# Preparation of the next block in thirds, and dequantisation gathered at the end of a layer, in a four-layer hybrid kernel

## The chip, the cores and the metric

The kernel runs on one core of one Trainium2 chip. The metric is the device time of one execution in microseconds (us): the median of the runs shown. A core has TensorE (PE, matrix products; its weight loads are listed apart as PEld), VectorE (DVE), ScalarE (ACT), GpSimd (POOL) and SyncE (SP, which here only issues DMAs). Each engine runs its own instructions in the order in which the program gives them, and they meet through semaphores. PE writes only PSUM; SBUF holds all other tiles.

## What is computed

One sequence of 2048 tokens with 256 channels in float32 goes through four layers, each added to its input after a layer norm: attention a, a gated MLP, attention b, the same MLP again.

```python
x = x + attn_a(layernorm(x))   # 16 heads of 16, 4 key/value heads, rotary angles, biases, causal
x = x + ffn(layernorm(x))      # gate, up: 256 -> 2048, gelu(gate) * up, down: 2048 -> 256
x = x + attn_b(layernorm(x))   # 16 heads of 16, 16 key/value heads, no bias, causal
x = x + ffn(layernorm(x))      # the same weights
```

The MLP's three weight matrices come packed, one 4-bit code pair to an int32 and one scale for each 32 values, and are expanded in the kernel once, for both MLP layers:

```python
low, high = W_packed & 15, W_packed >> 4 & 15
vals = NVFP4_LUT[stack([low, high], -1).reshape(N, -1)]
W = (vals.reshape(N, K // 32, 32) * scales[:, :, None]).reshape(N, K)
```

## The kernel before

**Blocks and units.** The tokens are cut into four blocks of 512 (`NB`), the 16 heads into four groups of four (`NG`). An attention layer is a sequence of 16 units, block by block and in each block the groups 0 to 3; unit (b, g) works out softmax(scores) times values for the queries of block b and the heads of group g (`value_steps`, main steps: one for each key tile of 128 and each pair of heads, so 8, 16, 24 or 32 steps in block 0, 1, 2 or 3). A main step adds the negated row maximum to the scores in PSUM (L853), adds the scores (L858), has ACT take the exponential (L870), and one step later PE multiplies by the values (L838).

**The max pass.** The row maxima must be known before. While unit n runs its main steps, `max_steps` computes the scores of unit n+1 a first time (L758) and DVE reduces them (L770), 9, 17, 25 or 33 steps for a unit of block 0, 1, 2 or 3. So the fourth unit of a block already scores the next block's first group, which needs that block's queries, and in its last steps its keys. The layer's last unit has no unit after it and no max pass.

**Side steps.** `weave` runs main steps and a list of side steps together: after each main step as many side steps as keep the two lists level, with the last three main steps kept free of them. The side list is the max pass blended with `more`, a list that `run` composes for every unit:

- the output projection of the block before (`out_steps`, four steps, in a block's first unit);
- preparation of the next block (`prep_steps(b + 1)`): layer norm (statistics, root on POOL, four normalised tiles `xn`), in the first layer the rotary tables (copied by POOL, L481, turned by PE, L492), the transposes of x (`turn_x`, L466), then projections in column blocks c of 128. In the first layer each rotated block is one product with the weights and one with the swapped weights (L500), each multiplied by its table on DVE (L514), added on POOL (L519), split into a high half (ACT copy, L550) and a low half (DVE, L558), both written to DRAM by SP (L557, L561). Keys come back through eight POOL DMAs (`load_k`, L705), queries through eight SP DMAs for a group (`load_q`, L719). Values go from PSUM to their tile (`keep_value`). This is 31 steps in the first layer and 27 in the second;
- in the first layer dequantisation (`dequant_steps`, handed to `run` as `extra`): 12 tiles of six steps, 72 in all: `load` (codes by SP, L330; scales in eight POOL DMAs, L339), `lowest` (POOL takes the low bytes, L344), two `move`s (DVE bit operations, L355 to L361) and two `scaled` (DVE, L370). Each of their tiles has one buffer, so a load of scales waits for the previous tile's last `scaled`. The first eight tiles fill `wg` and `wu`; the last four are the down projection, which SP writes to DRAM (L399) and the MLP loads again as `wd`;
- in the last unit, `beside`: the 13 steps that prepare block 0 of the MLP (layer norm, then four transposes of `xn`, L1007, copied to `xnT` by ACT, L1008). They come behind everything else in the list.

**Space.** PSUM has three double banks `ps_s` for scores, one bank `ps_av` for the sums of a unit, and one bank `ps_m` that all side products, the transposes and the turned maxima share. Query tiles have three buffers.

**What goes where before the change.** Preparation is cut into 13, 13 and 5 steps (first layer) or 11, 11 and 5 (second) for the units g = 0, 1, 2 of a block. Dequantisation goes in equal shares of six steps, one whole tile, to each of the 12 units of blocks 1 to 3, as a run ahead of the unit's preparation steps. Each unit issues at its start the query load of the unit two ahead.

Of the kernel before, what the change touches and what calls it, by code (L numbers as in the profile page):

```python
# [27 lines left out]
NG = NH // 4  # L28
# [3 lines left out]
NB = S // TB  # L32
# [10 lines left out]
def weave(main, side, rest=0):  # L43


    done = 0
    for n, step in enumerate(main):
        first, *second = step if isinstance(step, tuple) else (step,)
        first()
        want = min(len(side), -(-(n + 1) * len(side) // max(1, len(main) - rest)))  # L50
        while done < want:
            side[done]()
            done += 1
        for f in second:
            f()
    while done < len(side):
        side[done]()
        done += 1


def blend(a, b):

    keyed = [((n + 0.5) / len(a), 0, n, f) for n, f in enumerate(a)]
    keyed += [((n + 0.5) / len(b), 1, n, f) for n, f in enumerate(b)]
    return [f for *_, f in sorted(keyed, key=lambda k: k[:3])]


def cut(steps, n):

    while 0 < n < len(steps) and getattr(steps[n - 1], "open", False):  # L70
        n += 1
    return steps[:n], steps[n:]
# [8 lines left out]
def tile_hybrid_layers(  # L81
# [84 lines left out]
    for src, at in ((bq, 0), (bk, D), (bv, D + 64)):  # L166
        n = src.shape[1]
# [239 lines left out]
    class Attention:  # L407
# [535 lines left out]
        def run(self, extra, beside):  # L943


            units = [(b, g) for b in range(NB) for g in range(NG)]
            per_unit = -(-len(extra) // (len(units) - NG))
            ending, ahead = [], []
            for n, (b, g) in enumerate(units):
                lead, more = [], []  # L950
                if g == 0 and b > 0:
                    more += self.out_steps(b - 1)
                if g == 0 and b + 1 < NB:
                    ahead = self.prep_steps(b + 1)

                    few = -(-(len(ahead) - (6 if self.first else 5)) // 2)
                if n >= NG:
                    more, extra = more + extra[:per_unit], extra[per_unit:]
                if g < 3:
                    part, ahead = cut(ahead, few)  # L960
                    more += part
                if n == 0 and self.after:
                    lead, more = self.after[:2], self.after[2:] + more
                elif n + 2 < len(units):
                    self.load_q(*units[n + 2])
                maxima, turn = [], None
                if n + 1 < len(units):
                    maxima, turn = self.max_steps(*units[n + 1])
                else:
                    more += beside  # L970
                steps, end, divide = self.value_steps(b, g)

                for at, step in zip((0, 2), ending):
                    scored, *summed = steps[at] if isinstance(steps[at], tuple) else (steps[at],)
                    steps[at] = (scored, step, *summed)
                if turn:
                    scored, summed = steps[-1]
                    steps[-1] = (turn, scored, summed)
                first = len(maxima) * 3 // len(steps)
                weave(steps[:3], lead + maxima[:first])  # L980
                weave(steps[3:], blend(maxima[first:], more) if maxima else more, rest=3)
                ending = [end, divide]
            end()
            return [divide] + self.out_steps(NB - 1)
# [197 lines left out]
```

## Time and profile before

| | |
|---|---|
| median of 3 runs | 1878.29 us (1876.99 to 1888.44) |
| the profiled execution, its own time | 1879.59 us |
| its span, first to last instruction | 1877.8 us |
| mean granted PE clock | 0.988 |
| first attention layer, 16 units | 39.7 to 627.8 us |
| second attention layer, 16 units | 986.3 to 1534.7 us |

Times in a view count from the span's first instruction. The granted clock is the share of PE's full speed that the chip's throttle allowed in a stretch; it takes the values 1 and 0.5 here, so a mean of 0.98 over a stretch says that a small part of it ran at half speed. "Busy" of an engine is the time with an instruction of it under way; matmuls overlap, and their ends are modelled.

### The profile page before, as it was taken

How to read it: one execution, taken by the hardware profiler on the slowest of the kernel's cores; microseconds unless marked ns; L12 is line 12 of the kernel's file. 1: busy time of each engine (PE TensorE's matmuls, PEld its weight loads, DVE VectorE, ACT ScalarE, POOL GpSimd, SP SyncE). 2: the span in 40 equal slices, each digit the busy share in tenths (PEclk: the TensorE clock that was granted, in tenths of full speed). 3: DMA queues.
4: the chain of work that ended last, by engine and by line, in shares of the span. 5: the costliest groups of instructions: out<-in, count | busy, mean ns of one | idle time of the engine just before them, and what ended most of it. 6: DMA issues, size and time to landing. Idle time of an engine off the chain costs nothing. (4 is left out here: it accounts for less than half of the span.)

```text
span 1877.8 us, 31994 instructions
## 1 busy us (share of the span) xinstructions
PE 1774.6 (95%) x13534; PEld 928.5 (49%) x13534; DVE 1123.9 (60%) x1679; ACT 806.6 (43%) x1071; POOL 239.1 (13%) x444
## 2 busy tenths in 40 slices
PE   8788988999999999999998898999999999999999
PEld 4343444444444465646464444444444444756656
DVE  4566788688885354353544667766877716353443
ACT  1244445455667422232314355556566663131221
POOL 4211411300001011012101010010000001011110
PEclk9899999999999999999999899999999999999999
DMA  5320410310101100003204132041000010000000
GB/s 136 74 58 24 79 41 23 63 35 24 35 24 36 46 6 1 0 1 72 52 0 91 46 72 54 13 81 41 17 13 2 2 46 1 12 3 9 6 6 12
DMA packets 41887, 63.45 MB, mean 34 GB/s; under 512 B 13712, under 2 KB 20752, under 8 KB 41488
## 3 DMA queue, kind: packets, MB, share of 16 engines
q1 hardware_dynamic: 33104, 45.41, 8.6%
q0 software_dynamic: 7680, 15.48, 5.0%
q8 instruction: 106, 1.74, 0.4%
q10 hardware_dynamic: 960, 0.52, 0.1%
q14 instruction: 37, 0.30, 0.1%
HBM read 43.45 MB, written 17.83 MB: 33 GB/s over the span
## 5 line engine op out<-in xcount | busy, mean ns | idle before, releaser
L770 DVE TENSOR_REDUCE mx<-ps_s 128x2 f32<-128x1024 f32 (+3 forms) x640 | 658.7, 1060 | 220.0 <-PE ps_s L733 112.1
L870 ACT ACTIVATE e<-ps_s 128x1024 f32<-128x1024 f32 (+3 forms) x640 | 571.7, 898 | 423.4 <-PE ps_s L858 242.8
L838 PE MATMUL ps_av<-e,v 128*32 128x256 f32 (+1 forms) x4608 | 363.4, 384 | 0.4 <-ACT e L870 0.4
L858 PE MATMUL ps_s<-qT,kT 64*128 64x512 f32 (+3 forms) x1280 | 338.9, 522 | 0.0
L758 PE MATMUL ps_s<-kT,qT 64*128 64x512 f32 (+3 forms) x1280 | 268.2, 421 | 46.1 <-DVE mx L770 24.2
L853 PE MATMUL ps_s<-mT,sel 64*128 64x512 bf16 (+3 forms) x1280 | 231.0, 355 | 27.5 <-ACT mT L812 11.0
L1031 PE MATMUL ps_s<-xnT,wg 128*128 128x512 f32 x512 | 240.9, 593 | 0.0
L1031 PE MATMUL ps_s<-xnT,wu 128*128 128x512 f32 x512 | 240.6, 592 | 0.0
L758 PEld LDWEIGHTS ps_s<-kT,qT 64*128 64x128 f32 x1280 | 128.6, 187 | 151.9 <-ACT e L870 68.5
L853 PEld LDWEIGHTS <-sel 64*128 64x128 bf16 x1280 | 74.7, 93 | 251.6 <-issue 242.5
L1039 DVE TENSOR_TENSOR t<-ps_s,t 128x512 f32<-128x512 f32 x128 | 88.1, 688 | 158.8 <-POOL t L1038 156.7
L1037 ACT ACTIVATE t<-ps_s 128x512 f32<-128x512 f32 x128 | 76.2, 596 | 244.3 <-PE ps_s L1031 243.9
L1040 ACT ACTIVATE t<-t 128x512 f32<-128x512 f32 x128 | 80.5, 629 | 199.1 <-DVE t L1039 199.1
L1031 PEld LDWEIGHTS ps_s<-xnT,wu 128*128 128x128 f32 x512 | 97.3, 190 | 122.5 <-issue 122.5
L1038 POOL TENSOR_SCALAR t<-t 128x512 f32<-128x512 f32 x128 | 79.1, 618 | 565.4 <-ACT t L1037 564.9
L838 PEld LDWEIGHTS ps_av<-e,v 128*32 128x32 f32 x4608 | 94.6, 108 | 107.2 <-issue 91.7
L1031 PEld LDWEIGHTS ps_s<-xnT,wg 128*128 128x128 f32 x512 | 95.1, 190 | 104.2 <-issue 102.5
L1041 DVE SCALAR_TENSOR_TENSOR t<-t,ps_s 128x512 f32<-128x512 f32 x128 | 88.1, 688 | 88.9 <-ACT t L1040 88.9
L858 PEld LDWEIGHTS ps_s<-qT,kT 64*128 64x128 f32 x1280 | 129.5, 197 | 0.0
L1056 PE MATMUL ps_m<-wd,inter 128*128 128x256 f32 x512 | 114.5, 380 | 0.0
L1056 PE MATMUL ps_av<-wd,inter 128*128 128x256 f32 x512 | 114.5, 380 | 0.0
L1056 PEld LDWEIGHTS ps_av<-wd,inter 128*128 128x128 f32 x512 | 96.7, 190 | 17.1 <-issue 4.5
(145 smaller groups left out, 1201.3 us busy)
## 6 DMA issues: line engine op xcount, KB each, us to landing
qT<-h SPq DMA_DIRECT2D x248, 64.0 KB, 2.2
kT<-h POOLq DMA_DIRECT2D x88, 128.0 KB, 6.0
h<-high SPq DMA_DIRECT2D x24, 256.0 KB, 2.4
h<-low SPq DMA_DIRECT2D x24, 256.0 KB, 3.0
wd<-wd_kept SPq DMA_DIRECT2D x2, 2048.0 KB, 8.4
wd_kept<-dq_d SPq DMA_DIRECT2D x4, 512.0 KB, 3.0
out<-x SPq DMA_DIRECT2D x16, 128.0 KB, 1.7
x<-x SPq DMA_DIRECT2D x3, 512.0 KB, 7.3
```

Of the source, the lines that this page charges most:

```text
L758: nc.tensor.matmul(pt[:, r, :w], lhsT=self.qT[b, g][64 * r : 64 * r + 64, p, i * P : (i + 1) * P], rhs=self.key_rows(c, g, p, r, slice(0, w)),
L770: nc.vector.tensor_reduce(held["mx"][:, i, 2 * p : 2 * p + 2, c], pt[:, :, :w], AX.X, ALU.max)
L838: nc.tensor.matmul(held["av"][32 * j : 32 * j + 32, own], lhsT=self.vv[kt // NT][:, kt % NT, h * VW : h * VW + 32], rhs=es_[j // 2][:, j % ...
L853: nc.tensor.matmul(pt[:, r, q0:], lhsT=sel[64 * r : 64 * r + 64, p, :], rhs=self.mT[b, g][64 * r : 64 * r + 64, q0:], start=True, stop=False,)
L858: nc.tensor.matmul(pt[:, r, q0:], lhsT=self.key_rows(kt // NT, g, p, r, keys), rhs=self.qT[b, g][64 * r : 64 * r + 64, p, q0:], start=Fals ...
L870: nc.scalar.activation(e[:, :, q0:], pt[:, :, q0:], AF.Exp, scale=QK_SCALE)
L1031: nc.tensor.matmul(pt[:, k, :], lhsT=w[:, c, fc * P : (fc + 1) * P], rhs=self.xnT[b][:, c, :], start=(c == 0), stop=(c == 1),)
L1038: nc.gpsimd.tensor_scalar(t, t, GELU_A, 1.0, ALU.mult, ALU.add)
L1039: nc.vector.tensor_tensor(t, gate, t, ALU.mult)
L1040: nc.scalar.activation(t, t, AF.Tanh, scale=GELU_C)
L1041: nc.vector.scalar_tensor_tensor(t, t, 1.0, gate, ALU.add, ALU.mult)
L1056: nc.tensor.matmul(po[:, :D], lhsT=inter[:, fc, i * P : (i + 1) * P], rhs=wd[:, fc, :], start=(fc == 0), stop=(fc == NFC - 1),)
```

## The change

The edit is in `run` of the attention class alone.

- The preparation of the next block is cut into thirds: 8 or 9 steps in unit g = 0 (8 in block 0), 11 in g = 1, the rest, 11 or 12, in g = 2, in the first layer; 7 or 8, 11 or 10, and 9 in the second.
- The query load of unit (b + 1, 0) is no longer issued at the start of unit (b, 2), since the queries are now made in that unit: it stands as a step of its own after the sixth preparation step there.
- Dequantisation is shared by weights: none in block 0, 2 for each unit of blocks 1 to 3, but 0 for the fourth units of blocks 1 and 2, and 9 for the layer's last unit. Worked out, the 12 units of blocks 1 to 3 get 6, 5, 5, 0; 6, 5, 5, 0; 6, 5, 5, 24 steps. A tile's six steps may now lie in two units.
- The unit's share is blended into the list of preparation and output steps instead of standing ahead of it.

```diff
             units = [(b, g) for b in range(NB) for g in range(NG)]
-            per_unit = -(-len(extra) // (len(units) - NG))
-            ending, ahead = [], []
+            room = [0 if n < NG else 9 if n + 1 == len(units) else 2 * (g < 3 or b + 1 == NB)
+                    for n, (b, g) in enumerate(units)]
+            shares = [-(-len(extra) * sum(room[: n + 1]) // sum(room)) for n in range(len(units))]
+            given, ending, ahead = 0, [], []
             for n, (b, g) in enumerate(units):
                 lead, more = [], []
                 if g == 0 and b > 0:
                     more += self.out_steps(b - 1)
                 if g == 0 and b + 1 < NB:
                     ahead = self.prep_steps(b + 1)
-                    few = -(-(len(ahead) - (6 if self.first else 5)) // 2)
-                if n >= NG:
-                    more, extra = more + extra[:per_unit], extra[per_unit:]
-                if g < 3:
-                    part, ahead = cut(ahead, few)
+                    third = len(ahead) / 3
+                    few = [round(third) - (1 if b else 2), round(third) + 1, len(ahead)]
+                if g < 3 and b + 1 < NB:
+                    part, ahead = cut(ahead, few[g])
+                    if g == 2:
+                        part[6:6] = [lambda b=b: self.load_q(b + 1, 0)]
                     more += part
+                if shares[n] > given:
+                    more = blend(more, extra[given : shares[n]])
+                    given = shares[n]
                 if n == 0 and self.after:
                     lead, more = self.after[:2], self.after[2:] + more
-                elif n + 2 < len(units):
+                elif n + 2 < len(units) and g != 2:
                     self.load_q(*units[n + 2])
```

## The prediction

> **What bounds the kernel now.** I write unit (b, g) for the value pass of block b, head group g; a layer has 16, and each starts where ACT copies the previous unit's sums out of PSUM (L885). First the page's busy times and its row of slices:
>
> ```profile
> PE 1774.6 (95%) x13534; PEld 928.5 (49%) x13534; DVE 1123.9 (60%) x1679; ACT 806.6 (43%) x1071; POOL 239.1 (13%) x444
> ...
> PEclk9899999999999999999999899999999999999999
> ```
>
> PE is busy 95% of the span. The change moves work and removes none, so at most it can shift PE's idle time and the half-clock stretches; the question is which units have some. So I cut both attention layers into stretches (view of busy time by window; columns: window, length, then PE, PEld, DVE, ACT, POOL busy, granted clock, DMA share, GB/s). Units (1,0) to (1,2), (2,0) to (2,2) and the last, (3,3), of the first layer:
>
> ```profile
> 132.90:237.10 104.20, 91.08 (x920) 44.82 (x919) 71.89 (x122) 48.60 (x65) 26.24 (x45) 0.98 0.26 54
> ...
> 268.30:403.20 134.90, 124.30 (x1256) 58.06 (x1255) 99.57 (x146) 72.66 (x88) 26.42 (x45) 1.00 0.20 42
> ...
> 590.20:627.80 37.60, 37.12 (x405) 14.87 (x402) 6.65 (x23) 30.69 (x38) 1.04 (x1) 1.00 0.04 15
> ```
>
> The same two stretches of the second layer, whose preparation is lighter and which has no dequantisation:
>
> ```profile
> 1068.40:1159.10 90.70, 85.41 (x906) 43.24 (x903) 59.53 (x89) 48.61 (x66) 9.16 (x17) 1.00 0.32 65
> ...
> 1188.80:1313.20 124.40, 118.54 (x1240) 57.43 (x1239) 87.58 (x113) 73.15 (x90) 9.17 (x17) 1.00 0.22 48
> ```
>
> PE's idle time is length less PE: 13.1 and 10.6 us in the first layer, 5.3 and 5.9 in the second. In (3,3) PE idles 0.5 and DVE 31: there PE sets the pace. The fourth units (1,3) and (2,3), each first in layer 1, then in layer 2:
>
> ```profile
> 237.10:268.30 31.20, 25.78 (x298) 12.69 (x297) 28.38 (x40) 14.77 (x19) 4.42 (x9) 1.00 0.13 35
> 1159.10:1188.80 29.70, 25.21 (x298) 12.61 (x297) 26.04 (x32) 14.76 (x20) 0.00 (x0) 1.00 0.07 17
> 403.20:444.70 41.50, 36.53 (x410) 17.23 (x409) 37.75 (x48) 23.03 (x28) 4.62 (x9) 1.00 0.10 27
> 1313.20:1353.00 39.80, 36.52 (x410) 17.05 (x409) 35.47 (x40) 22.91 (x27) 0.00 (x0) 1.00 0.05 13
> ```
>
> Here DVE is busy nearly throughout (28.38 of 31.20): the next block's longer max pass. Last, what PE waits for in (1,0) to (1,2) (us, times, longest):
>
> ```profile
> PE ps_s L758 <- ACT e L870: 3.1, 5, 1.2
> PE ps_s L758 <- DVE mx L770: 2.4, 3, 1.1
> PE ps_m L500 <- DVE r L514: 1.5, 2, 0.8
> ```
>
> Exponentials behind other ACT work, max reductions behind other DVE work, and the single `ps_m` bank. All three come from side steps set too densely.
>
> **Part A, no dequantisation in (1,3) and (2,3).** After the edit these units hold what their twins of the second layer hold, so they take the twins' length: 31.20 - 29.70 = 1.5 and 41.50 - 39.80 = 1.7. **-3.2**. DVE loses 2.34 and 2.28 busy, so -4.6 is the lower end, 0 the upper. Late next: the max reductions themselves, which stay.
>
> **Part B, thirds, blocks 1 and 2 of the first layer.** Before, unit g=1 held 13 preparation steps, eight using `ps_m`, g=2 five (two). Now it is 9, 11 and 11 steps, and preparation uses `ps_m` seven times in g=1 and five in g=2. Dequantisation, which stood in a lump ahead of them, is mixed in. PE's instructions are the same. At best idle falls to the second layer's level: 23.7 - 11.2 = -12.5. I take a little over half, **-7**, since the heavier preparation (swapped columns, tables) stays. Upper end +3: a load of scales is eight issues on POOL, 3.97 us, and can stand ahead of POOL's add L519, for which ACT's copy L550 waits with the next exponentials behind it. By the lists the copy comes three or more main steps (over 5 us) after each such load, and the eight key loads (0.51 each, 4.1) no longer wait in line for their DRAM write, made a unit earlier; so I keep near the gain. The query load's eight issues leave the head of g=2 for its middle; in SP's queue they now stand behind the halves' writes, with ten or more us to spare in blocks 1 and 2.
>
> **Part C, block 0 of both layers, and the second layer's thirds.** Block 0's units have 8 main steps, and all side work lands in two of them, wherever it is moved; idle there is 15.1 us of 72.2 (first layer) and 8.1 of 60.0. In the second layer two transposes of x leave g=0, one projection leaves g=1; its six other units idle 11.2, of which about 1 each is the fixed wait for mT and o. **-2** for all of it; ends -7, and +10 (second rival). Block 3's units g=0 to 2 go from 18 dequantisation steps to 16, beside DVE's 29 us of idle: 0.
>
> **Part D, the last unit.** By the new shares unit (3,3) gets 24 of the 72 steps, four whole tiles, against one before; ahead of the MLP's own 13 steps, in the same 26 main steps. DVE has 31 us free and four tiles cost it 4 x 2.7. But tiles of a stage have one buffer each, so the four go one after the other. One tile's round, from POOL's and DVE's timelines (start, length):
>
> ```profile
> 582.94 3.97 POOL L339 DMA_DIRECT2D dq_s<-down_s  x8 [41.23 <-DVE dq_d L370]
> 588.19 0.61 POOL L344 COPY dq_b<-dq_q 128x512 uint8<-128x512 uint8 x1 [1.28 <-DMA dq_q<-down_p]
> ```
>
> ```profile
> 581.96 0.68 DVE L370 SCALAR_TENSOR_TENSOR dq_d<-dq_e,dq_s 128x512 f32<-128x512 fp8e4 x1
> ...
> 592.18 0.21 DVE L355 TENSOR_SCALAR dq_t<-dq_b 128x128 uint32<-128x128 uint32 x1
> ...
> 593.56 1.29 DVE L370 SCALAR_TENSOR_TENSOR dq_d<-dq_e,dq_s 128x512 f32<-128x512 fp8e4 x2
> 594.78 0.42 DVE L295 BATCH_NORM_STATS2 stats<-x 128x6 f32<-128x256 f32 x1
> ...
> 598.36 1.38 DVE L310 TENSOR_SCALAR xn<-x,mv,rstd 128x256 f32<-128x256 f32 x4 [1.16 <-POOL rstd L302]
> ```
>
> From the last scaling's start (581.96) to the next tile's unpacked bytes (588.80) it takes 6.84; from there to its own last scaling 2.0 (592.18 to 594.17). Period: 8.8. The first tile is loaded ahead and ends as it does now, last scaling at T+3.97 (T = 590.2); the fourth starts its last at T+30.4; statistics 0.6 later; the first normalised x 4.0 after that: **T+35.0**. PE now reaches the transposes of it (L1007) here:
>
> ```profile
> 616.46 0.50 PE L1007 MATMUL ps_m<-ident,xn 128*128 128x128 f32 x2
> ...
> 620.38 0.34 PE L853 MATMUL ps_s<-mT,sel 64*128 64x384 bf16 x2
> ```
>
> With 37 side steps in place of 19 the first transpose moves from main step 24 to 27, the one that starts at 620.38; less the two transposes that no longer precede it (0.9) and plus its scores (0.45), PE stands there at T+29.75. It waits about **5.0** for DVE, with all later scores and the MLP's first matmuls queued behind. Two transposes now share that step and one bank: +0.9. And the clock: in 176.87 to 180.28 PE was busy 1.82 of 3.41 us, and the next 3.41 ran at 0.50; a stall of 5 us leaves at least one such window emptier than that. Half clock for 3.4 to 6.8 us over a stretch where PE sets the pace costs 1.7 to 3.4: +2.5. **+8.4**; ends 0 and +13 (landings at their longest, 4.6 and 5.0). The write of the last down tile and the 2 MB load of `wd` slip by 27 us, but the first down projection comes some 60 us after the unit.
>
> [...]
>
> **Sum.** -3.2 - 7 - 2 + 8.4 = -3.8 on the profiled execution's 1879.59 (span 1877.8): 1875.8. That execution stands 1.3 above the median of the runs, so **1874.5**.
>
> **Rivals.** *The clock holds through the stall*: D is 5.9, 1872, inside the forecast's own range (0.12 of its chance): for it the window 1542.18 to 1545.59, PE busy 1.99, with the next at 1.00; against it the emptier one above.
> *The last unit hides it all* (chance 0.15): if a round takes 7.06 or less, x is ready at T+29.75 and nothing of D is paid: 1874.5 - 8.4 = 1866. For it: DVE's 31 idle us, and landing rows as short as 1.9. Against: two rounds in the trace are 8.65 and 8.85, mostly fixed issues.
> *Thirds give nothing* (0.18): the idle moves from g=1 to g=2 along with `ps_m`'s users; B and C are 0: 1883.5, slower. For it: the three waits above are local to a step, not to a unit.
> *Block 0's queries come late* (0.10): (0,2) loads what (0,3) scores at once. Modelled on (0,1), where the low half (81.0) was followed by key loads, add and next halves up to the write at 89.5, then 3.0 landing, four issues of 0.46 and 2.2 landing: 15.6 us after it, U+20.5 in a unit of about 22 whose successor reads at U+23. It decides if a landing is over 2.5 us longer than its median; the query rows reach 8.0. Then 3.4 us of stall and 1.7 of half clock, in both layers: +10, 1884.5, slower.
> That the change doesn't do what it says shows only in the word "mostly": a third of the dequantisation goes to the last unit.
>
> **The numbers.** The forecast (1868 to 1881) has 0.50; 0.07 lies outside all of these. The range reaches from the first rival with part of B's best (1862) to D's upper end or the slower rivals with a little more (1888). About 1%, 18.8 us, is what a measurement of this kernel can tell from no change; no case passes it without two bounds at once: faster 0.04, within 0.89, slower 0.07.
>
> **What would show it.** A: (1,3) and (2,3) at 29.7 and 39.8. B: idle of the two first-layer stretches near 16 to 17 in all. D: PE waiting several us for xn at L1007 near the end of the last unit, the clock at 0.5 behind it, POOL's eight issues starting every 8.8 us. C: the first L758 of (0,3) waiting for qT or not. The prediction is wrong if the rounds overlap, if clock windows in block 0 fall differently (each 3.4 us there costs up to 1.7), or if mixing slows the max reductions in the first three units.

## The result

| | before | changed |
|---|---|---|
| median (9 runs each, side by side) | 1882.21 us | 1869.66 us |
| range of the runs | 1876.99 to 1889.71 | 1865.59 to 1874.91 |
| the profiled execution | 1879.59 (granted clock 0.988) | 1874.91 (0.983) |

The ratio of changed to before is 0.9935, 95% interval 0.9913 to 0.9957: 12 us faster, within 1%. The forecast was 3.8 us faster, 1874.5. The two profiles differ by only 4.7 us; they were taken at unlike clocks, and more on that stands below.

The page after, the lines that answer to those shown of before:

```profile
PE 1779.5 (95%) x13534; PEld 929.9 (50%) x13534; DVE 1124.8 (60%) x1679; ACT 806.5 (43%) x1071; POOL 240.3 (13%) x444
...
PEclk9879999999999899999999899999999999999999
```

The first layer by stretches (window, length, then busy time of PE, PEld, DVE, ACT and POOL, granted clock, DMA share, GB/s): units (1,0) to (1,2), (1,3), (2,0) to (2,2), (2,3), and the last unit.

```profile
133.60:230.00 96.40, 88.89 (x920) 44.19 (x919) 69.61 (x120) 48.31 (x64) 22.88 (x37) 1.00 0.23 56
230.00:259.80 29.80, 25.22 (x298) 12.61 (x297) 26.11 (x32) 14.80 (x20) 0.00 (x0) 1.00 0.07 20
259.80:389.20 129.40, 123.03 (x1256) 57.84 (x1255) 98.08 (x140) 72.73 (x89) 26.22 (x45) 1.00 0.16 44
389.20:429.10 39.90, 36.65 (x410) 17.04 (x409) 35.58 (x40) 22.84 (x27) 0.00 (x0) 1.00 0.05 14
...
575.40:623.80 48.40, 40.93 (x405) 15.74 (x402) 14.20 (x47) 30.69 (x38) 14.80 (x28) 0.86 0.23 77
```

The first three units of blocks 1 and 2 fell from 104.2 and 134.9 to 96.4 and 129.4, **-13.3**. The fourth units fell by 1.4 and 1.6, **-3.0**, to their twins' length. The last unit grew from 37.6 to 48.4, **+10.8**, at a granted clock of 0.86. Everything else changed by little in these two profiles: block 0 93.2 to 94.0, block 3's first three units 145.5 to 146.3, the second layer 548.5 to 548.1.

The last unit, by PE's waits and its timeline:

```profile
PE ps_m L1016 <- DVE xn L310: 6.5, 1, 6.5
```

```profile
604.93 0.47 PE L858 MATMUL ps_s<-qT,kT 64*128 64x384 f32 x2
611.93 0.70 PE L1016 MATMUL ps_m<-ident,xn 128*128 128x128 f32 x2 [6.53 <-DVE xn L310]
```

PE stands at the transposes (L1016 is the earlier L1007) from T+30.0 (605.40 in a unit that starts at 575.4) and gets its x at T+36.5. POOL's timeline shows why, three rounds of scales, bytes, and the wait in front of each:

```profile
580.29 3.97 POOL L339 DMA_DIRECT2D dq_s<-down_s  x8 [7.78 <-DVE dq_d L370]
586.68 0.61 POOL L344 COPY dq_b<-dq_q 128x512 uint8<-128x512 uint8 x1 [2.42 <-DMA dq_q<-down_p]
590.32 3.97 POOL L339 DMA_DIRECT2D dq_s<-down_s  x8 [3.02 <-DVE dq_d L370]
595.45 0.61 POOL L344 COPY dq_b<-dq_q 128x512 uint8<-128x512 uint8 x1 [1.16 <-DMA dq_q<-down_p]
599.43 3.97 POOL L339 DMA_DIRECT2D dq_s<-down_s  x8 [3.37 <-DVE dq_d L370]
```

Each load of scales waits for the previous tile's last scaling on DVE: rounds of 10.0 and 9.1 us (580.29, 590.32, 599.43).

### The profile page after: what moved, and what is told of

It reads as the page before. It is cut to its first block, busy times and chain, and to the rows that moved or that the text cites. A ratio compares the mean times of both kernels' runs of the same rounds, so it can differ in the third digit from the quotient of the medians.

```text
span 1873.1 us, 31992 instructions
## 1 busy us (share of the span) xinstructions
PE 1779.5 (95%) x13534; PEld 929.9 (50%) x13534; DVE 1124.8 (60%) x1679; ACT 806.5 (43%) x1071; POOL 240.3 (13%) x444
## 5 line engine op out<-in xcount | busy, mean ns | idle before, releaser
L758 PEld LDWEIGHTS ps_s<-kT,qT 64*128 64x128 f32 x1280 | 129.4, 189 | 137.7 <-ACT e L870 67.6
L1040 PEld LDWEIGHTS ps_s<-xnT,wu 128*128 128x128 f32 x512 | 97.3, 190 | 122.5 <-issue 122.5
L1040 PEld LDWEIGHTS ps_s<-xnT,wg 128*128 128x128 f32 x512 | 95.1, 190 | 104.2 <-issue 102.5
L838 PEld LDWEIGHTS ps_av<-e,v 128*32 128x32 f32 x4608 | 94.9, 109 | 104.2 <-issue 87.9
## 6 DMA issues: line engine op xcount, KB each, us to landing
kT<-h POOLq DMA_DIRECT2D x88, 128.0 KB, 5.0
out<-x SPq DMA_DIRECT2D x16, 128.0 KB, 1.7
```

What stands on the lines that cost most here:

```text
L758: nc.tensor.matmul(pt[:, r, :w], lhsT=self.qT[b, g][64 * r : 64 * r + 64, p, i * P : (i + 1) * P], rhs=self.key_rows(c, g, p, r, slice(0, w)),
L838: nc.tensor.matmul(held["av"][32 * j : 32 * j + 32, own], lhsT=self.vv[kt // NT][:, kt % NT, h * VW : h * VW + 32], rhs=es_[j // 2][:, j % ...
L1040: nc.tensor.matmul(pt[:, k, :], lhsT=w[:, c, fc * P : (fc + 1) * P], rhs=self.xnT[b][:, c, :], start=(c == 0), stop=(c == 1),)
```

## The experiments

Twelve kernels ran in three sets, each set beside the kernel before on one chip; its median was 1881.0 in the first set, 1884.4 in the second, 1881.3 in the third. The theory taken from the prediction: thirds make the gain, the order on DVE makes the loss.

**Thirds alone.**

```diff
...
-                if shares[n] > given:
-                    more = blend(more, extra[given : shares[n]])
-                    given = shares[n]
+                if n >= NG:
+                    outs = 4 if g == 0 else 0
+                    more, extra = more[:outs] + extra[:per_unit] + more[outs:], extra[per_unit:]
```

> Preparation in thirds as in the change, dequantisation left as before (six steps, one tile, in each unit of blocks 1 to 3, ahead of the preparation). Theory (the thirds themselves make the gain): the stretches of units (1,0) to (1,2) and (2,0) to (2,2) of the first layer fall by 10 us or more of the 13.4 that the whole change took off them; the fourth units stay at 31.2 and 41.4, the last at 37.6; total 10 to 14 us under the kernel before, ratio 0.993 to 0.995. Rival (mixing dequantisation into the preparation makes the gain): the two stretches fall by under 4 us, ratio 0.998 or more.

**Shares and mixing alone**: the new shares and the blending, put into the kernel before.

> Dequantisation by the new shares and mixed in, preparation left in 13, 13 and 5 steps. Theory: the two stretches fall by 3 us or so, the fourth units by 1.5 each, the last unit grows by 10.8 through its wait: 3 to 6 us over the kernel before, ratio 1.002 to 1.003. Rival (mixing makes the gain): the stretches fall by 10 or more, ratio 0.997 or less.

Measured, 1871.31 (ratio 0.994, 0.9919 to 0.9961) and 1879.59 (0.9982, 0.9963 to 1.0001). The stretches, thirds alone:

```profile
133.15:233.85 100.70, 89.85 (x920) 44.75 (x919) 70.34 (x122) 48.64 (x65) 26.12 (x45) 1.00 0.24 56
265.05:399.35 134.30, 123.26 (x1256) 58.53 (x1255) 98.13 (x146) 72.80 (x89) 26.13 (x45) 1.00 0.18 42
```

and shares and mixing alone:

```profile
138.60:236.20 97.60, 88.96 (x920) 44.06 (x919) 69.44 (x120) 48.47 (x65) 22.68 (x37) 1.00 0.25 55
265.90:396.40 130.50, 122.93 (x1256) 58.08 (x1255) 98.14 (x140) 72.70 (x88) 26.29 (x45) 1.00 0.19 44
```

Thirds take 4.1 off the two stretches, the other half of the edit takes 11.0. The theory fell: in these stretches the rival is right, or nearly so (it allowed the thirds under 4). The ratios are less clear. That of the first run lies where the theory put it, because thirds also shorten block 0 and its last unit stays at 37.6. The total of the second run is kept up by its last unit (45.4 us): stretches, fourth units and last unit come to -6, and its interval reaches -7.

**Mixing alone, equal shares**, to part mixing from the smaller shares:

```diff
-                if n >= NG:
-                    more, extra = more + extra[:per_unit], extra[per_unit:]
                 if g < 3:
                     part, ahead = cut(ahead, few)
                     more += part
+                if n >= NG:
+                    more, extra = blend(more, extra[:per_unit]), extra[per_unit:]
```

> The kernel before with one thing changed: each unit's six dequantisation steps are blended into its preparation and output steps instead of standing ahead of them. Shares, halves and the last unit's order stay. Theory now (a run of DVE steps at the head of a unit lets DVE set the pace there while PE starves, and the preparation behind it then lets PE set the pace while DVE starves; mixing evens the two out): the two stretches of units g=0 to 2 of blocks 1 and 2 fall by 8 to 11 us in sum, the fourth units stay at 31.2 and 41.4 and the last at 37.6; ratio 0.993 to 0.996. Rival (the smaller shares of five steps, not the mixing, made the gain of the run with new shares and halves): they fall by under 4 us, ratio 0.998 or more.

**The run behind the preparation**: the same, with `more + extra[:per_unit]` in place of the blend.

> The kernel before with each unit's six dequantisation steps in one run behind the preparation instead of ahead of it. Theory (uneven load, wherever the run stands): the starved stretch moves to the unit's end, the two stretches of units fall by under 4 us in sum, ratio 0.997 to 1.002. Rival (the place at the unit's head is the cause: the tile's codes are loaded there behind the eight query loads, so its bytes come late): they fall by 8 us or more, ratio under 0.996.

Mixing alone: 1872.07, ratio 0.9937 (0.9925 to 0.9949), as much as the whole change; the stretches 97.3 and 130.3, -11.5. The smaller shares add nothing to that (97.6 and 130.5 above). What mixing does is seen at the head of unit (2,1). Before, from some 1.4 us into the unit, the 14 us with the run of dequantisation and the 24 us behind it:

```profile
314.00:328.00 14.00, 11.17 (x106) 4.85 (x106) 13.27 (x20) 7.22 (x8) 0.61 (x1) 1.00 0.11 33
328.00:352.00 24.00, 23.12 (x168) 9.24 (x166) 12.35 (x15) 9.64 (x11) 6.59 (x10) 1.00 0.24 40
```

The same places of the unit with mixing alone:

```profile
307.40:321.40 14.00, 13.82 (x102) 5.48 (x102) 10.19 (x12) 7.03 (x9) 0.62 (x1) 1.00 0.10 32
321.40:345.40 24.00, 22.81 (x216) 9.71 (x212) 17.61 (x27) 11.23 (x13) 6.65 (x10) 1.00 0.38 67
```

Before, DVE is full (13.27 of 14) and PE has 2.8 us of holes; then PE is nearly full and DVE half idle. Mixed, PE stands 0.2 and 1.2 us in the two. The heads of (1,1), (1,2) and (2,1) together make 5.6 of the 7.7 us of PE's idle time that mixing takes off the two stretches. Not every head is like that. The same 14 us of (1,2) before and with mixing alone, then of (2,2) before:

```profile
211.30:225.30 14.00, 11.76 (x126) 5.96 (x126) 12.72 (x22) 6.41 (x8) 4.86 (x9) 1.00 0.28 42
207.10:221.10 14.00, 13.61 (x146) 7.11 (x147) 12.35 (x22) 8.20 (x10) 3.76 (x6) 1.00 0.33 80
366.30:380.30 14.00, 13.76 (x126) 5.55 (x130) 13.41 (x19) 8.67 (x10) 3.36 (x5) 1.00 0.24 38
```

In (2,2) DVE is as full, and PE idles 0.2 us only. So it is shown that mixing makes this gain; that a full DVE starves PE is read from some of the heads and does not hold in each.

The run behind the preparation should have been neutral by this theory and a gain by the rival. It was neither: 1894.37, ratio 1.0047 (1.0032 to 1.0063), stretches 112.8 and 137.0. Its DVE and POOL in unit (1,1):

```profile
214.12 1.41 DVE L355 TENSOR_SCALAR dq_t<-dq_b 128x128 uint32<-128x128 uint32 x1 [4.43 <-POOL dq_b L344]
```

```profile
208.38 1.28 POOL L519 TENSOR_TENSOR r<-r 128x512 f32<-128x512 f32 x1 [6.16 <-DVE r L514]
209.60 3.87 POOL L339 DMA_DIRECT2D dq_s<-up_s  x8
213.47 0.62 POOL L344 COPY dq_b<-dq_q 128x512 uint8<-128x512 uint8 x1
```

Behind the preparation, POOL can't run ahead: its add (L519) comes first, then eight issues, then the bytes, and DVE, already at its `move`, waits 4.43 us with the max reductions behind it; PE waits 4.6 for those, and from 214.94 the clock is at half for 10.2 us. This suggests a second condition: load and use of a tile must lie apart on POOL as well, which mixing does too. It rests on two such waits in this run:

```profile
DVE dq_t L355 <- POOL dq_b L344: 7.2, 2, 4.4
```

In the kernel before DVE waits for these bytes 0.07 us at most, so the rival's reason, bytes that come late at the unit's head, is out by that profile.

**The MLP's preparation first in the last unit**, the rest as changed:

```diff
-                    more += beside
+                    more = beside + more
```

> The whole change, but in the layer's last unit the 13 steps that prepare the MLP stand ahead of the 24 dequantisation steps instead of behind them (both layers' last units use the same line; the second has no dequantisation). Theory (DVE's order is the cause: the normalised x waits behind four serial tiles): the last unit falls from 48.4 to 37.6 to 38.5 and PE waits for nothing at the transposes; 10 to 11 us under the changed kernel, ratio to the kernel before 0.986 to 0.989. Rival (the amount of dequantisation beside the exponentials costs, wherever it stands): the unit stays over 44.

**The stall filled.**

```diff
+                    if self.first:
+                        beside[-4:-4] = [lambda: idling(30)]
                     more += beside
...
+    def idling(n):
+        pt = ps_m()
+        for _ in range(n):
+            nc.tensor.matmul(pt, lhsT=sel[:, 0, :], rhs=nothing, start=True, stop=True)
```

> The whole change, with 30 matmuls of zeros (128x512, bf16, some 6.5 us) on PE just ahead of the transposes in the first layer's last unit, where PE stands still for 6.5 us. Theory (the unit's 10.8 us are 6.5 of stall and some 4 of half clock after it): the stall's time is filled, the clock stays at 1.0, the unit takes 43 to 45 us in place of 48.4. Rival (half clock costs nothing there, since PE then waits for the exponentials or for the single bank): the unit stays at 48 or grows.

The last unit of the first, then of the second:

```profile
571.10:609.60 38.50, 37.02 (x405) 14.75 (x401) 14.04 (x47) 30.61 (x37) 19.66 (x37) 1.00 0.30 90
```

```profile
574.50:619.50 45.00, 44.00 (x434) 17.76 (x431) 14.20 (x47) 30.65 (x37) 14.86 (x28) 1.00 0.25 83
```

With the same 24 steps beside it, but behind the MLP's, the unit takes 38.5: order, not amount. Total 1861.12, ratio 0.9889 (0.9862 to 0.9917); PE's longest wait there is 1.0, for the single bank. Filled, the clock stays at 1.00 and the unit takes 45.0, which is 37.6 + 6.5 + 0.9: the filled time, and the shared bank as in the first run (38.5 - 37.6). The half clock behind the stall therefore cost about 48.4 - 45.0 = 3.4 in the first profile. The total, 1868.73 (0.9925, 0.9902 to 0.9949), can't be told from the changed kernel's.

**What thirds are worth once all is mixed**: halves, with the new shares, mixing and the MLP first.

> Dequantisation by the new shares and mixed, the MLP's preparation first in the last unit, and preparation left in 13, 13 and 5 steps: beside the run with thirds and the same last unit (ratio 0.989) it prices the thirds alone. Theory (thirds are the lesser part): the two stretches stand at 97 to 98 and 130 to 131 against 96.4 and 129.3, block 0 of the first layer idles 17 to 18 us on PE against 14 to 16; ratio 0.991 to 0.994. Rival (thirds are nothing once all is mixed): ratio 0.989 or less.

**Halves in block 0's units only**, and, in the same set, thirds throughout, both with the MLP's preparation first as above, and the changed kernel itself again:

```diff
+                    if b == 0:
+                        half = -(-(len(ahead) - (6 if self.first else 5)) // 2)
+                        few = [half, half, len(ahead)]
...
-                    if g == 2:
+                    if g == 2 and b > 0:
...
-                elif n + 2 < len(units) and g != 2:
+                elif n + 2 < len(units) and (g != 2 or b == 0):
```

> The whole change with the MLP's preparation first in the last unit, but the preparation of block 1 (done in block 0's units, in both layers) cut into halves as before, with the query load back at the start of the third unit. Theory (thirds earn in block 0 of the first layer, where all side work falls on two main steps): PE's idle time in that block goes back from 15 to 18 us, its length from 91 to 94 up to 94 to 100 (the clock's half windows there differ from run to run), block 0 of the second layer from 13 to 11 us of idle; 2 to 5 us over the run with thirds throughout, of the same call. Rival (what thirds earn lies in blocks 1 and 2 alone): no difference over 1 us.

> The whole change with the MLP's preparation first in the last unit once more, for comparison within one call: ratio 0.988 to 0.990, last unit 38.5, 8 to 10 us under the changed kernel of the same call.

> The changed kernel itself once more, for the same call and for a second profile. Theory (the first profile met more half-clock windows than most executions): where the granted clock is higher than 0.983 the span is shorter by about 1.2 us for each 0.001; the stretches of units (1,0) to (1,2), (2,0) to (2,2) and the fourth units stay within 0.3 us of 96.4, 129.4, 29.8 and 39.9; the last unit lies between 44.9 (stall alone) and 48.4, block 0 between 91 and 94. Rival (the profiled time is the usual one): the span stays at 1873.

Halves throughout: 1870.88, 0.9929 (0.9918 to 0.9941); stretches 97.6 and 130.5. Halves in block 0 only: 1868.74, 0.9933 (0.9914 to 0.9951). Thirds throughout: 1864.32, 0.9918 (0.9903 to 0.9932), short of the expected ratio and 5.7 under the changed kernel of the same set instead of 8 to 10, but 4.4 under the run with halves in block 0 (the two intervals overlap, and the means of the six runs each lie 2.9 apart). Block 0 of the first layer, with halves and with thirds:

```profile
40.20:140.10 99.90, 81.38 (x762) 42.64 (x765) 53.91 (x97) 31.91 (x50) 16.71 (x26) 0.81 0.24 55
```

```profile
40.00:133.10 93.10, 78.17 (x762) 41.33 (x765) 53.87 (x97) 31.99 (x50) 17.15 (x26) 0.85 0.25 59
```

PE's idle time is 18.5 against 14.9, as expected. So thirds earn most in block 0 of the first layer. There all profiles with halves give 93.2 to 99.9 (six, mean 97.4), those with thirds 91.2 to 94.0 (eight, mean 92.7): -4.7, which the first pair of profiles hid, since its "before" was the shortest of the six.

The changed kernel again: 1870.06, 0.9947 (0.9932 to 0.9962), profiled at clock 0.986 with a span of 1869.3. The stretches were 96.4, 129.3, 29.7, 39.9, block 0 93.1, and the last unit:

```profile
574.90:621.30 46.40, 40.06 (x405) 15.34 (x402) 14.20 (x47) 30.69 (x38) 14.86 (x28) 0.89 0.26 81
```

```profile
PE ps_m L1016 <- DVE xn L310: 5.4, 1, 5.4
```

So the last unit costs +8.8 or +10.8. About half of the difference is the stall itself, 5.4 us here and 6.5 in the first profile; the rest goes with the half clock, 10.2 us here and 13.7 there.

**Lighter shares in blocks 1 and 2**, MLP first; then with the last unit's weight cut from 9 to 6 (the edit shown is the second):

```diff
-            room = [0 if n < NG else 9 if n + 1 == len(units) else 2 * (g < 3 or b + 1 == NB)
+            room = [0 if n < NG else 6 if n + 1 == len(units) else (1 if b + 1 < NB else 3) * (g < 3)
```

> The whole change with the MLP's preparation first in the last unit, and lighter shares in blocks 1 and 2: weights 1 in their first three units and 3 in those of block 3, so 3 steps each there, 9 in block 3, 27 in the last unit. If DVE's load beside PE still costs in blocks 1 and 2, the two stretches fall by 2 to 4 us against the changed kernel's 96.4 and 129.4 and block 3's grow by under 1: ratio 0.986 to 0.988. If mixing has taken all there is, the stretches stay within 1 us and the ratio is that of the run with the MLP's preparation first, 0.989.

> As the run with light shares in blocks 1 and 2 (3 steps a unit) and the MLP's preparation first, but with the last unit's weight cut from 9 to 6: 11 or 10 steps in each of block 3's first three units, 20 in the last. Theory (27 steps were too many: the output's division in the MLP's first features waited 2.6 us behind the chain, and the clock fell after it): the MLP takes 358.5 again and the total falls by 2 to 3 us under that run, ratio 0.985 to 0.987. Rival (the wait came from elsewhere): the MLP stays at 361.

With 9: 1859.64, 0.9873 (0.9861 to 0.9886); stretches 96.0 and 128.0, only 1.8 less than the changed kernel's, and a new wait in the MLP's first features:

```profile
PE ps_m L920 <- DVE att L900: 2.6, 1, 2.6
```

With 6, the MLP takes 358.5 again as expected (361.4 with 9) and the total is 1859.64, 0.9892 (0.9876 to 0.9907): the same median, 21.7 under the kernel before of its set and 10.4 under the changed kernel of the same set. The expected ratio, 0.985 to 0.987, was not reached, and the further 2 to 3 us did not come. The two share the lowest median of this study.

## Why the prediction was right, and where it was not

The sign and the range held; the size did not: 3.8 forecast, about 12 measured. By its steps:

| part | forecast | measured |
|---|---|---|
| A, fourth units | -3.2 | -3.0 |
| B, units 0 to 2 of blocks 1 and 2 | -7 | -13.3 |
| C, block 0, block 3, second layer | -2 | +1.2 in the first pair; near -5 by all profiles |
| D, last unit | +8.4 | +10.8 and +8.8 |

**A** was right by the twins, and its cause is confirmed: with thirds alone, where the fourth units keep their six steps, they stay at 31.2 and 41.5.

**B was mis-sized twice.** The lower end, -12.5, counted only PE's idle time. PE's *busy* time shrank as well: from 91.1 and 124.3 to 88.9 and 123.0, 3.5 us. The half-clock window after 180.28 stood in it, and doing without it can be at most 1.7 of that; where the rest comes from is open. And "a little over half" of the idle time was too little: idle went from 23.7 to 13.9, 9.8 of the 12.5. The step also put the weight on the wrong part. It named the density of `ps_m`'s users in g=1 first; mixing alone gives -11.5, thirds alone -4.1. The hint was in the profile: 7.4 of the 23.7 us of idle sat in 14 us at the heads of (1,1), (1,2) and (2,1), and windows of that length show it; the stretches over three units that the prediction used average it away. The price of POOL's order, up to +3 there, did not fall due with mixing; the run with the tile behind the preparation shows one of that kind, 4.4 us of wait and then the clock.

**C.** The loss that its rival feared, late queries in (0,3), did not come: none of PE's waits there, in either layer, is for a query load. The two longest in the first:

```profile
PE ps_s L758 <- DVE mx L770: 1.9, 3, 1.1
PE ps_s L853 <- DVE mx L770: 1.2, 2, 0.7
```

The gain in block 0 of the first layer was undersized, since I took the idle time of 8-step units to be the same wherever the steps go. In the third unit PE instead waits 2.0 us at the values' product for the single bank, in the second layer 1.6. In the first layer that is less than what the other two units save. In the second it is not: PE's idle time in block 0 rises from 11.1 to 13.0 us in the first pair (11.4 to 13.3 as means), and thirds gain nothing there.

**D held in mechanism and nearly in size.** PE arrived at T+30.0 (forecast T+29.75); x came at T+36.5, not T+35.0, because two of the three rounds took 10.0 and 9.1 in place of 8.8; in the first the codes landed late (2.42 us of POOL's wait). The clock fell, as the emptier-window reading had it; the rival in which it holds is out. It fell at 608.04, 2.6 us into the stall. The window of 3.41 us ahead of that, and what followed:

```profile
604.63:608.04 3.41, 0.77 (x12) 0.21 (x4) 2.58 (x9) 0.89 (x1) 0.61 (x1) 1.00 0.01 2
608.04:611.46 3.42, 0.00 (x0) 0.00 (x0) 2.10 (x9) 0.00 (x0) 1.04 (x1) 0.50 0.38 153
```

So the clock fell here after a window in which PE had been busy 0.77 us. PE's busy time in a window gives no sharp rule: in the kernel before the clock also fell after one with 2.27 us busy, while it held after the one with 1.99 that the prediction names:

```profile
118.84:122.25 3.41, 2.27 (x36) 1.49 (x36) 3.20 (x6) 0.81 (x1) 0.00 (x0) 1.00 0.00 0
122.25:125.66 3.41, 3.38 (x39) 2.10 (x35) 2.75 (x4) 0.60 (x1) 0.00 (x0) 0.50 0.02 5
```

Behind the stall the half clock lasted 9.8 us, not 3.4 to 6.8, and cost about 3.4, not 2.5. The rival that the last unit hides everything would have been right with one line in another place, as the run with the MLP first shows.

**The base** was the last error. The forecast was set against an execution at a clock of 0.988 and a median of three, 1878.29, where nine runs have 1882.21. Counted from there its inner band, 1868 to 1881, would have been 1872 to 1885, and 1869.66 lies under that: that the time itself fell into the band is luck. The 41 further executions of the kernel before give 1881.5 on average at 0.986 (ten of them), and eight of the changed kernel at the same clock 1870.1: 11.4 apart. The parts by all profiles come to the same: A -3.0, B -13.3, C -5.0 (block 0 of the first layer -4.7 and of the second +0.3, as means; the second layer's other units -1.4, block 3 +0.8), D +9.8 as the mean of two, -11.5 in all.

## What to carry to other kernels

Where side work is woven into a main loop, mix the steps of different engines instead of laying them in runs: here a run of DVE steps filled DVE (13.27 of 14 us at the head of (2,1)) while PE had holes (2.8 us), and the next stretch was the reverse (DVE 12.35 of 24 us, PE 23.12), while averages over the unit show neither. Read such a loop in windows shorter than a unit. What was put last in a stage with idle engines stood behind everything queued there (PE waited 6.5 us for it, and 1.0 at most once it came first): put first what the bound engine will wait for, and let a serial chain of single-buffered tiles run out behind it.

## What the runs showed of the hardware

The spread of this kernel's time goes with the granted clock. Over 41 executions of the kernel before (one more, of 4096.6 us, is left out) the time follows the mean clock almost on a line, 1875.7 us at 0.992 to 1893.6 at 0.977, about 1.2 us for each 0.001. The same instructions of block 0 took 93.2 us in the profile of the kernel before (clock 0.89 there) and 99.9 in that of the run with shares and mixing alone (0.79), which differ only from block 1 on:

```profile
39.70:132.90 93.20, 75.06 (x766) 39.59 (x765) 53.78 (x97) 31.82 (x50) 16.73 (x26) 0.89 0.25 59
```

```profile
38.70:138.60 99.90, 82.31 (x762) 43.17 (x765) 53.88 (x97) 31.88 (x49) 16.75 (x26) 0.79 0.23 55
```

Some DVE operations also took longer beside POOL. In the run with the tile behind the preparation the 128x128 TENSOR_SCALAR shown above took 1.41 us, against 0.21 elsewhere, and the next two instructions 0.75 and 0.71, against 0.22 and 0.29, while POOL did its four adds of the output bias (2.75 us from 214.04). That is 2.2 us of the 4.6 that PE waited there. It is not a single case. In the kernel before, a small DVE operation ended together with an add of POOL:

```profile
360.47 1.09 DVE L791 TENSOR_TENSOR rest<-nm,m_pad 128x16 f32<-128x16 f32 x1
360.20 1.32 POOL L519 TENSOR_TENSOR r<-r 128x512 f32<-128x512 f32 x1 [8.58 <-DVE nm L782]
```

In the profiles of the kernel before and of the change this operation took 0.18 us in 63 cases and 1.09 in the one that overlaps with a computing instruction of POOL. Beside POOL's four adds of the output bias (2.80 us from 216.17 in the kernel before), L357 and L361 took 0.77 and 0.72 us, against 0.22 and 0.29 elsewhere in that profile. The max reductions of 1024 scores, which read PSUM, took 1.22 us in the 33 such overlaps of the two profiles as elsewhere. Why some take longer beside POOL and others do not is not shown by these runs.
